# Two more row sums taken off ScalarE, and one small copy that holds the waits of four exponentials, in an attention kernel bound by TensorE

## The chip, the cores and the metric

The kernel runs on one core of a Trainium2 chip. The metric is the device time of one execution in microseconds (us), lower is better. Before the change the median of three runs is 656.49 us (655.96 to 656.77). All data is float32, apart from some bfloat16 helper tiles.

## The reference

Attention with a condition token, added to its input. Eight batches (the weights' setup names 4, but x has 8), 512 positions, 512 channels in 16 heads of 32.

```python
Q = _split_heads(x @ Wq.T + bq)
K = _split_heads(x @ Wk.T + bk)
V = _split_heads(x @ Wv.T + bv)
cQ = Q + tQ     # tQ, tK: the token, through the same weights
cK = K + tK
scores = jnp.einsum('bhqd,bhkd->bhqk', cQ, cK) / jnp.sqrt(jnp.float32(HEAD_DIM))
attn = jax.nn.softmax(scores, axis=-1)
out = jnp.einsum('bhqk,bhkd->bhqd', attn, V)
x = x + out.transpose(0, 2, 1, 3).reshape(B, S, D_MODEL)
```

## The kernel before

The work is cut into T = 32 steps t = 0 to 31: a batch times a group of four heads (one head on each 32 of the 128 partitions). The engines' instruction order is written out by hand (a manual schedule); the loop of the middle part runs over t = 1 to 28. A step has four items, here called its **quarters** i = 0 to 3. In each quarter TensorE does four things one after the other: for even t the scores of step t, keys on partitions (`exponentials`, L808 and L811); the scores of the next step's rows, queries on partitions (`row_max` with `row_scores`, L672 for even t, L664 for odd t); and either the product of the previous step's weights with V (L833) or a part of the projections of the batch ahead (L473).

The rows (u, qc) of a step u, 128 queries times four heads j, need three things. VectorE takes the negated row maximum out of PSUM (L628, L681). ScalarE takes exp(score - maximum), with the maximum as its bias (`denominators`, L729). And somebody sums each row. ScalarE can do that in the same instruction (`accum_out`), and then a second ScalarE instruction, ACTIVATION_READ_ACCUMULATOR, follows, which the profile lists under the same line.

Even and odd steps differ in what becomes of that exponential. For a **blocked** step (odd u from 1 to 27) it is kept: it is written into eight of the 14 rooms of the SBUF tile `arena`, and DMAs (`exchange`, L703) move it from there into `blocks`, 24 on the queue of SyncE and 8 on that of GpSimd in each step, half of them for the query quarters 0 and 1 and half for 2 and 3. VectorE turns blocks of 32 x 32 in place (`turn_blocks`, L692), and the result is multiplied with V. For the other steps the exponentials of the rows are thrown away after their sum, and L822 makes them again from the scores with keys on partitions; these take two rooms for each quarter. In an even step t the fourth quarter's L822 writes rooms 0 and 1, which the exchange of step t+1 has read (its first half, g = 0 and 1).

The rows of the blocked steps u = 3 to 27 are made in the even steps t = u - 1 (t = 2 to 26, thirteen of them): their row (u, 0) in the last quarter of step t - 1, and (u, 1), (u, 2), (u, 3) in the quarters 0, 1 and 2 of step t. ScalarE is a queue: behind a quarter's L822 come the four L729 of the rows, and these free the PSUM banks that a later quarter's L672 writes. Thus the exponentials of (u, 2) are read out of their banks while TensorE nears the L672 of the quarter i = 2, and those of (u, 3) before the L672 of i = 3.

Three tables say who sums the rows of blocked steps (u from 3):

```python
BY_VECTOR = {0: [(0, 0)], 1: [(2, 0), (2, 1)], 2: [(3, 0), (3, 1)]}
IN_PART = {0: (0, 1), 1: (2, 2)}
PART_AT = {0: 0, 1: 2}
```

`BY_VECTOR` names heads (qc, j) that VectorE sums from `arena` (L756) in the quarter of the key. `IN_PART` names two that GpSimd adds up in part: three adds (L746) bring 512 columns down to 128, in a free corner of the weight tile `wT_k` called `part`; VectorE then sums those 128 (L751) in the quarter that `PART_AT` gives. All other heads of the sixteen, (0,2), (0,3), the four of qc 1, (2,3), (3,2) and (3,3), are summed by ScalarE.

An instruction that has several semaphores to wait for gets separate EVENT_SEMAPHORE instructions ahead of it on its engine's queue.

Of the kernel before, what the change touches and what calls it, by code (L numbers as in the profile page):

```python
# [12 lines left out]
ALU = mybir.AluOpType  # L13
AX = mybir.AxisListType
# [3 lines left out]
def kernel(  # L18
# [38 lines left out]
    nc = tc.nc  # L57
    P = 128
# [4 lines left out]
    HG = P // HD  # L63
# [219 lines left out]
    table = const.tile([P, 1], F32, tag="table", name="table")  # L283
# [21 lines left out]
    for h in range(HG):  # L305
        r = slice(h * P, (h + 1) * P)
# [17 lines left out]
    for i in range(NS):  # L324
        r = slice(i * BL, (i + 1) * BL)
# [8 lines left out]
    def in_place(b):  # L334
# [5 lines left out]
    wT = {  # L340
        n: const.tile([P, NC, D], F32, tag=f"wT{n}", name=f"wT_{n}") for n in ("q", "k", "v")
    }
# [277 lines left out]
    sums = {}  # L620
# [66 lines left out]
    def turn_blocks(t, units):  # L687

        for n in units:
            pr = slice(n % NP * 2, n % NP * 2 + 2)  # L690
            e = blocked[t][:, :, n // NP, pr, :].rearrange("p g h s -> p g (h s)")
            nc.vector.transpose(e, e)  # L692

    def exchange(t, half):

        if t not in blocked:
            blocked[t] = room(f"blocks_{t}")
        for g in range(HG):
            for a in range(HG):
                queue = nc.gpsimd if a in BY_POOL else nc.sync  # L700
                of = arena[a * BL : (a + 1) * BL, half * HG + g, :]
                to = blocked[t][g * BL : (g + 1) * BL, a, half * 2 : half * 2 + 2]
                queue.dma_start(to.rearrange("p c h s -> p (c h s)"), of)  # L703

    APART = [(1, 1, 3), (1, 3, 3), (29, 2, 2), (29, 2, 3)]
    apart_rooms = {}
# [1 line left out]
    def denominators(t, qc, w=HG, js=range(HG)):  # L708

        if t >= T - 2:  # L710
            return
        for j in js:
            if t in BLOCKED:
                to = rows_kept(t, qc // 2)[:, :, qc % 2, j, :].rearrange(
                    "p g (c e) -> p g c e", e=BL
                )
            elif (t, qc, j) in APART:
                to = apart_rooms[j] = arena[:, (place[0] + 6) % ROOMS, j % 2 * S : j % 2 * S + S]
            else:
# [4 lines left out]
            by_vector = (  # L724
                (t, qc, j) in APART
                if t == 1 or t not in BLOCKED
                else any((qc, j) in a for a in BY_VECTOR.values()) or (qc, j) in IN_PART.values()
            )
            nc.scalar.activation(  # L729
                to,  # L730
                of,
                AF.Exp,
                bias=nmax[t][:, qc, j, :],
                **({} if by_vector else {"accum_out": sums[t][:, qc, j, :]}),
            )
            if by_vector and (qc, j) == IN_PART.get(0):
                sum_in_part(t, qc, j)

    part = wT["k"][:, 0:2, P + P // 2 : 2 * P]

    def sum_in_part(t, qc, j):

        if t in BLOCKED:
            e = rows_kept(t, qc // 2)[:, :, qc % 2, j, :].rearrange("p g (i s) -> p g i s", i=2)
            for g in range(1, HG):
                nc.gpsimd.tensor_tensor(part, part if g > 1 else e[:, 0], e[:, g], ALU.add)  # L746

    def sum_part(t, qc, j):

        if t in BLOCKED:  # L750
            nc.vector.tensor_reduce(sums[t][:, qc, j, :], part, AX.XY, ALU.add)  # L751

    def sum_by_vector(t, qc, j):

# [439 lines left out]

    def more_sums(t, i):

        for k, at in PART_AT.items():
            if at == i:
                sum_part(t + 1, *IN_PART[k])
        for qc, j in BY_VECTOR.get(i, ()):  # L1200
            sum_by_vector(t + 1, qc, j)

    for t in range(1, T - 3):
        b, r = divmod(t, G)
        blocks = t in BLOCKED
        w = 0 if blocks else HG
        items = ["V", "q", "k", "v"] if blocks else ["V", "k", "q", "v"]
        for i, item in enumerate(items):
            rows = (t + 1, i + 1) if i < 3 else (t + 2, 0)
            begin(w)  # L1210
            if not blocks:
                exponentials(t, i)
            late_first = item in ("v" if blocks else "qkv") and t % 2 == 1
            hold = row_max(*rows, late_first, w, not blocks and item in SINGLY)

            def held(i=i, hold=hold):
                hold()
                if i == 2:
                    split_max(t + 1)
                    turn_max(t + 1)  # L1220

            dens = lambda js=range(HG): denominators(*rows, w, js)
            if item in "qkv":
                products(t, item, blocks, held, dens, nothing)
            else:
                held()
                dens()
                if blocks:
                    weighted(t - 1, banks(4), banks(5), nothing)
                    released(6, 7, 0, 1, 2, 3, 5, 4)  # L1230
                else:
                    weighted(t - 1, banks(0), banks(1), lambda: more_sums(t, 0))
                    released(2, 3, 1, 4, 5, 6, 7, 0)
            if i == 0 and r % 2 == 0:
                turn_x(t + NC + 2)
                turn_x(t + NC + 3)
            if i == 0 and r == 1:
                combine_x(b + 1, 1, nc.gpsimd)
            if i == 1 and r == 0:
                combine_x(b + 1, 0, nc.gpsimd)  # L1240
            if i == 2:
                aparts[t] = masked(t)
            turn_more(t, i)
            if not blocks:
                if t == T - 4 and i == 1:
                    for j in apart_rooms:
                        nc.vector.tensor_reduce(
                            sums[t + 1][:, 2, j, :], apart_rooms[j], AX.X, ALU.add
                        )
                if i:  # L1250
                    more_sums(t, i)
                if i in IN_PART and i:
                    sum_in_part(t + 1, *IN_PART[i])
            for what in ORDERS[t % 2, i]:
                if what == "store":
                    store()
                elif what == "residual":
                    if 3 < t + 1 <= T - 4:
                        load_residual(t + 1)
                elif what == "x":  # L1260
                    load_pairs()
                elif t + 1 in BLOCKED:
                    exchange(t + 1, what)
    row_of[0] = None

    def latest_pair(of, among):
# [64 lines left out]
    t = T - 3  # L1331
# [25 lines left out]
    t = T - 2  # L1357
# [25 lines left out]
    t = T - 1  # L1383
# [61 lines left out]
    b, g = divmod(t, G)  # L1445
# [55 lines left out]
```

## Time and profile before

| | before |
|---|---|
| median of 3 runs | 656.49 us |
| the profiled execution: time, span | 656.52 us, 654.4 us |
| busy: TensorE, VectorE, ScalarE, GpSimd | 99%, 93%, 82%, 60% of the span |
| granted TensorE clock | 0.999 |
| the even step t = 14 (315.86 to 336.04), the odd one after it | 20.18 us, 18.58 us |

The span runs from the first to the last instruction; the 2.1 us between span and time lie around it. PE is TensorE's matmuls, PEld its weight loads, DVE is VectorE, ACT ScalarE, POOL GpSimd, SPq the queue of SyncE. A float32 matmul leaves two records. A row of the timeline holds the start in us, the length in us, engine, line, operation, tiles written and read, shapes and the number of instructions merged; in brackets follow the engine's idle time just before it and what ended it. Matmul records overlap, so a wait of TensorE is best seen in the time from the start of one group to the start of the next.

### The profile page before, as it was taken

To read this page: it belongs to the slowest core of one execution; us is meant where nothing else is said; L and a number is where in the kernel's file an instruction comes from. 1 tells how busy PE (TensorE), PEld (TensorE's weight loads), DVE (VectorE), ACT (ScalarE), POOL (GpSimd) and SP (SyncE) were. 2 spreads that over 40 slices of the span, in tenths; PEclk is the share of its full clock that TensorE was granted. 3 is DMA by queue.
4 is the path that set the end of the run, shared out by engine and by line. 5 is a ranking of instruction groups with operands and counts; after the bars stand their busy time and mean duration, and the time that the engine had idled before them with its cause. 6 is when DMAs were issued, how large, how long until landed. Compare 5 with 4: busy or idle time off the path is not lost.

```text
span 654.4 us, 24011 instructions
## 1 busy us (share of the span) xinstructions
PE 646.6 (99%) x9568; PEld 308.2 (47%) x9568; DVE 610.0 (93%) x911; ACT 535.5 (82%) x1298; POOL 391.6 (60%) x555
## 2 busy tenths in 40 slices
PE   8999999999999999999999999999999999999997
PEld 6444453544535454454545445454554545445432
DVE  4899999999999999999999999999999999997786
ACT  2589798888988888888989889788897988889664
POOL 4653564768647676586746766476864766555440
PEclk9999999999999999999999999999999999999999
DMA  9818549295675839758594865839567582940212
GB/s 201 159 35 214 120 105 218 62 219 129 152 176 119 210 80 212 153 130 195 95 220 93 189 159 136 200 80 221 116 158 176 123 202 49 221 106 7 53 33 33
DMA packets 140819, 90.92 MB, mean 139 GB/s; under 512 B 117436, under 2 KB 126308, under 8 KB 140708
## 3 DMA queue, kind: packets, MB, share of 16 engines
q1 hardware_dynamic: 133252, 73.91, 50.7%
q0 software_dynamic: 5568, 14.95, 9.3%
q8 instruction: 75, 1.23, 0.8%
q10 hardware_dynamic: 1888, 0.52, 0.3%
q14 instruction: 36, 0.29, 0.2%
HBM read 20.27 MB, written 8.39 MB: 44 GB/s over the span
## 4 chain that ended last, share of the span: by engine, by line
PE 97%; DMA 1%; DVE 1%; ACTq 0%; issue 0%; SPq 0%; DVEq 0%
PE psum L473 44%; PE psum L833 18%; PE psum L672 10%; PE psum L664 9%; PE psum L811 9%; PE psum L808 3%; PE psum L414 2%; DMA early<-in_x_dram 1%; PE psum L1307 1%; PE psum L1420 0%; PE psum L940 0%; PE psum L870 0%; DVE nmax L1325 0%; DVE nmax L681 0%; PE psum L792 0%; ACTq L250 0%
## 5 line engine op out<-in xcount | busy, mean ns | idle before, releaser
L628 DVE TENSOR_REDUCE nmax<-psum 128x1 f32<-128x512 f32 x326 | 204.8, 679 | 13.3 <-PE psum L672 7.9
L729 ACT ACTIVATE psum<-psum,nmax 128x512 f32<-128x512 f32 x254 | 167.8, 665 | 46.1 <-DVE nmax L628 33.9
L822 ACT ACTIVATE arena<-psum 128x512 f32<-128x512 f32 x264 | 136.3, 603 | 33.2 <-PE psum L811 26.0
L729 ACT ACTIVATE arena<-psum,nmax 128x512 f32<-128x512 f32 x226 | 146.9, 710 | 5.1 <-DVE nmax L628 3.7
L692 DVE STREAM_TRANSPOSE blocks<-blocks 128x1024 f32<-128x1024 f32 x112 | 132.2, 1217 | 0.7 <-issue 0.5
L681 DVE TENSOR_REDUCE nmax<-psum 128x2 f32<-128x1024 f32 x87 | 105.3, 1211 | 1.3 <-PE psum L672 1.3
L901 POOL TENSOR_TENSOR res<-res,recs 128x512 f32<-128x512 f32 x30 | 31.4, 1047 | 112.3 <-DVE res L900 112.3
L672 PE MATMUL psum<-kT,qT 32*128 32x512 f32 x576 | 83.1, 597 | 0.0
L833 PE MATMUL psum<-arena,v 128*32 128x512 f32 x576 | 68.5, 597 | 0.0
L811 PE MATMUL psum<-qT,kT 32*128 32x512 f32 x528 | 67.9, 587 | 0.0
L703 POOL DMA_DIRECT2D blocks<-arena x112 | 55.9, 505 | 17.7 <-PE psum L811 8.7
L664 PE MATMUL psum<-kT,qT 32*64 32x512 f32 x896 | 62.4, 613 | 0.0
L833 PE MATMUL psum<-blocks,v 128*32 128x256 f32 x896 | 52.6, 381 | 0.0
L672 PEld LDWEIGHTS psum<-kT,qT 32*128 32x128 f32 x576 | 39.4, 183 | 27.5 <-ACT arena L729 7.8
L729 ACT ACTIVATION_READ_ACCUMULATOR psum<-psum,nmax 128x1 f32 x254 | 52.3, 206 | 0.0
L756 DVE TENSOR_REDUCE sums<-arena 128x1 f32<-128x512 f32 x66 | 42.3, 673 | 0.4 <-ACT arena L729 0.4
L833 PEld LDWEIGHTS psum<-blocks,v 128*32 128x32 f32 x896 | 31.0, 110 | 20.8 <-ACT arena L822 10.6
L902 POOL TENSOR_TENSOR xr<-res,xr 128x512 f32<-128x512 f32 x30 | 38.5, 1282 | 2.4
L213 POOL TENSOR_TENSOR xr<-xr,wT_q 128x512 f32<-128x512 f32 x30 | 38.4, 1282 | 0.3
L473 PE MATMUL psum<-wT_v,xT 128*32 128x256 f32 x512 | 34.2, 382 | 0.0
L473 PE MATMUL psum<-wc_v,xc 128*32 128x256 f32 x512 | 33.5, 379 | 0.0
L833 PEld LDWEIGHTS psum<-arena,v 128*32 128x32 f32 x576 | 14.7, 110 | 38.0 <-issue 19.6
(199 smaller groups left out, 1097.8 us busy)
## 6 DMA issues: line engine op xcount, KB each, us to landing
blocks<-arena SPq DMA_DIRECT2D x336, 128.0 KB, 4.3
blocks<-arena POOLq DMA_DIRECT2D x112, 128.0 KB, 4.4
xr<-in_x_dram SPq DMA_DIRECT2D x60, 128.0 KB, 2.7
x<-in_x_dram SPq DMA_DIRECT2D x56, 128.0 KB, 2.7
out_dram<-xr SPq DMA_DIRECT2D x56, 128.0 KB, 3.1
w_q<-in_L_cond_Wq_dram SPq DMA_DIRECT2D x4, 256.0 KB
w_k<-in_L_cond_Wk_dram SPq DMA_DIRECT2D x4, 256.0 KB, 7.2
w_v<-in_L_cond_Wv_dram SPq DMA_DIRECT2D x4, 256.0 KB
```

The lines of the kernel that those rows point to most:

```text
L473: nc.tensor.matmul(pt[r], still[:, r], moving, start=(kc == kcs[0]), stop=(kc == kcs[-1]))
L628: nc.vector.tensor_reduce(nmax[t][:, qc, j : j + 1, 0], pt, AX.X, ALU.max, negate=True)
L664: nc.tensor.matmul(pt[i * n : (i + 1) * n], qkT["q", t][r, qc * P + i * n : qc * P + (i + 1) * n], qkT["k", t][r, :], start=True, stop=True,)
L672: nc.tensor.matmul(pt, qkT["q", t][r, qc * P : (qc + 1) * P], qkT["k", t][r, :], start=True, stop=True,)
L681: nc.vector.tensor_reduce(nmax[t][:, qc, pr * 2 : pr * 2 + 2, 0], pt, AX.X, ALU.max, negate=True)
L692: nc.vector.transpose(e, e)
L703: queue.dma_start(to.rearrange("p c h s -> p (c h s)"), of)
L729: nc.scalar.activation(to, of, AF.Exp, bias=nmax[t][:, qc, j, :], **({} if by_vector else {"accum_out": sums[t][:, qc, j, :]}),)
L756: nc.vector.tensor_reduce(sums[t][:, qc, j, :], rows_kept(t, qc // 2)[:, :, qc % 2, j, :], AX.XY, ALU.add)
L811: nc.tensor.matmul(bank[j], qkT["k", t][r, kc * P : (kc + 1) * P], qkT["q", t][r, :], start=False, stop=True,)
L822: nc.scalar.activation(e[:, i, :], bank[pr * 2 + i], AF.Exp)
L833: nc.tensor.matmul(pt[j * HD : (j + 1) * HD, at], vs[b % 2][:, kc, (g * HG + j) * HD : (g * HG + j + 1) * HD], e, start=(kc == chunks[0]), ...
```

## The change

Three things change, all for the blocked steps.

First, the tables. The heads (2,3) and (3,2) of the steps u = 3 to 27 are now summed in part by GpSimd, so that ScalarE's exponential of them has no `accum_out`. (2,3) gets a corner of `wT_k` of its own; (3,2) shares the one of (2,2). GpSimd adds (2,3) right behind (2,2) in the quarter i = 1, and (3,2) behind its four DMAs of the exchange's second half, in i = 2. VectorE finishes both in the quarter i = 0 of the odd step that follows, behind the transpose of the result (L900).

Second, `wait_ahead`. Behind the exponential of (u, 3, 3) ScalarE gets a copy of one column, `table` onto itself, which is made to wait for all who read or wrote the rooms 0 and 1: the eight DMAs of the exchange, GpSimd's adds, an earlier exponential. This happens in the step t = 0 too, for u = 1.

Third, `more_sums` is called in odd steps as well, and picks step and heads by the table.

```diff
-    IN_PART = {0: (0, 1), 1: (2, 2)}
-    PART_AT = {0: 0, 1: 2}
+    IN_PART = {0: [(0, 1)], 1: [(2, 2), (2, 3)], 2: [(3, 2)]}
+    PART_AT = {(0, 0): [(0, 1)], (0, 2): [(2, 2)], (1, 0): [(2, 3), (3, 2)]}
...
+    readers = []
+    def wait_ahead():
+        if readers:
+            ins = nc.scalar.copy(table, table).ins
+            for r in readers:
+                tc.add_manual_dep(
+                    ins,
+                    r.name,
+                    mybir.DependencyInfo(mybir.DependencyClass.Sync, mybir.DependencyReason.DATA),
+                    reason="rooms of the next exponentials",
+                )
+            readers.clear()
...
-                queue.dma_start(to.rearrange("p c h s -> p (c h s)"), of)
+                sent = queue.dma_start(to.rearrange("p c h s -> p (c h s)"), of)
+                if half == 0 and g < 2:
+                    readers.append(sent.ins)
...
+            if t in BLOCKED and (qc, j) == (1, HG - 1):
+                readers.append(made.ins)
+            if t in BLOCKED and (qc, j) == (3, HG - 1):
+                wait_ahead()
...
+            at = (P + P // 2, 3 * P)[j % 2 if qc else 0]
+            part_rooms[qc, j] = wT["k"][:, 0:2, at : at + P // 2]
...
-        for k, at in PART_AT.items():
-            if at == i:
-                sum_part(t + 1, *IN_PART[k])
+        u = t + 1 - t % 2
+        for qc, j in PART_AT.get((t % 2, i), ()):
+            if t > 1 or qc == 0:
+                sum_part(u, qc, j)
+        if t % 2:
+            return
...
-            if not blocks:
+            if blocks:
+                more_sums(t, i)
+            else:
...
                     exchange(t + 1, what)
+                    if what:
+                        for qc, j in IN_PART[2]:
+                            sum_in_part(t + 1, qc, j)
```

ScalarE, from the row exponentials of the quarter i = 1 of an even step (its row (u, 2)) to L822 of i = 3, before: L822 are the exponentials with keys on partitions, L729 those of the rows, `sums` in the output means a sum by ScalarE. The semaphores in brackets stand for DMAs (DMAHW on the queue of SyncE, DMASW on that of GpSimd) and engines.

```order
L729 ACTIVATE arena<-psum,nmax_3562 128x4x128 [waits DVE_49] x2
L729 ACTIVATE arena,sums_3563<-psum,nmax_3562 128x4x128 [waits DVE_49]
L822 ACTIVATE arena<-psum 128x512 [waits PE_49] x4
L729 ACTIVATE arena<-psum,nmax_3562 128x4x128 [waits DVE_49] x2
L729 ACTIVATE arena,sums_3563<-psum,nmax_3562 128x4x128 [waits DVE_49] x2
L822 ACTIVATE arena<-psum 128x512 [waits DMAHW0_49,DMASW6_49,DMAHW1_49,PE_49,DMAHW7_49,Activation_49,Pool_49]
L822 ACTIVATE arena<-psum 128x512 [waits PE_49,Activation_49]
L822 ACTIVATE arena<-psum 128x512 [waits DMAHW3_49,DMAHW2_49,DMAHW4_49,DMASW7_49,PE_49]
L822 ACTIVATE arena<-psum 128x512 [waits PE_49]
```

The same place now; L746 is the old L729, L853 the old L822, L699 the new copy.

```order
L746 ACTIVATE arena<-psum,nmax_3608 128x4x128 [waits DVE_49] x3
L853 ACTIVATE arena<-psum 128x512 [waits PE_49] x4
L746 ACTIVATE arena<-psum,nmax_3608 128x4x128 [waits DVE_49] x2
L746 ACTIVATE arena<-psum,nmax_3608 128x4x128 [waits DVE_49,Pool_49]
L746 ACTIVATE arena,sums_3609<-psum,nmax_3608 128x4x128 [waits DVE_49]
L699 COPY table<-table 128x1 [waits DMAHW1_49,DMAHW2_49,DMAHW0_49,DMAHW3_49,DMASW7_49,DMAHW4_49,DMASW6_49,DMAHW7_49,Activation_49,Pool_49]
L853 ACTIVATE arena<-psum 128x512 [waits PE_49] x4
```

The last head of the first group and the third head of the second have lost their sums, and the fourth quarter's exponentials wait for TensorE alone.

GpSimd, from the exchange's first half to its second and on, before, in an even step that also prepares the next batch (L397, L398; six of the thirteen):

```order
L703 DMA blocks_4702<-arena 32x1024 x4
L580 TENSOR_TENSOR kT_4522<-wT_k,kT_4522 128x256
L397 TENSOR_TENSOR xc<-xT_4199 128x512
L398 TENSOR_TENSOR xc<-xc,xT_4199 128x512
L746 TENSOR_TENSOR wT_k<-arena 128x2x64
L746 TENSOR_TENSOR wT_k<-wT_k,arena 128x2x64 x2
L580 TENSOR_TENSOR qT_4452<-wT_q,qT_4452 128x256
L860 TENSOR_TENSOR wT_k<-sums_4359,which 128x64
L703 DMA blocks_4702<-arena 32x1024 x4
L213 TENSOR_TENSOR xr_4627<-xr_4627,wT_q 128x16x32
L901 TENSOR_TENSOR res_4939<-res_4939,recs_4937 128x512
```

Now (L775 the adds, L718 the DMAs, L891 and L932 the old L860 and L901):

```order
L398 TENSOR_TENSOR xc<-xc,xT_4254 128x512
L775 TENSOR_TENSOR wT_k<-arena 128x2x64
L775 TENSOR_TENSOR wT_k<-wT_k,arena 128x2x64 x2
L775 TENSOR_TENSOR wT_k<-arena 128x2x64
L775 TENSOR_TENSOR wT_k<-wT_k,arena 128x2x64 x2
L580 TENSOR_TENSOR qT_4516<-wT_q,qT_4516 128x256
L891 TENSOR_TENSOR wT_k<-sums_4421,which 128x64
L718 DMA blocks_4766<-arena 32x1024 x4
L775 TENSOR_TENSOR wT_k<-arena 128x2x64
L775 TENSOR_TENSOR wT_k<-wT_k,arena 128x2x64 x2
L213 TENSOR_TENSOR xr_4691<-xr_4691,wT_q 128x16x32
L932 TENSOR_TENSOR res_5010<-res_5010,recs_5008 128x512
```

Three adds stand ahead of the second half's DMAs, and three behind them.

VectorE, at the start of an odd step, before (L681 and L628 are maxima, L900 the result's transpose):

```order
L681 TENSOR_REDUCE nmax_4358<-psum 128x2
L880 RECIPROCAL recs_4435<-psum 128x16
L900 STREAM_TRANSPOSE res_4437<-psum 128x512
L628 TENSOR_REDUCE nmax_4358<-psum 128x1 x2
L681 TENSOR_REDUCE nmax_4358<-psum 128x2
L692 STREAM_TRANSPOSE blocks_4202<-blocks_4202 128x4x256 x2
```

Now (L782 the old L751, L911 and L931 the old L880 and L900):

```order
L681 TENSOR_REDUCE nmax_4420<-psum 128x2
L911 RECIPROCAL recs_4497<-psum 128x16
L931 STREAM_TRANSPOSE res_4499<-psum 128x512
L782 TENSOR_REDUCE sums_4122<-wT_k 128x1 x2
L628 TENSOR_REDUCE nmax_4420<-psum 128x1 x2
L681 TENSOR_REDUCE nmax_4420<-psum 128x2
```

Two short sums have come in between the transpose and the maxima of the next quarter.

More of the change, by code (lines that the diff above doesn't have):

```diff
@@ L735, in denominators, with room_for_part @@
             )
[L736 removed]
+            if by_vector and (qc, j) in IN_PART[0]:
                 sum_in_part(t, qc, j)
[L739 removed]
+            if t in BLOCKED and (qc, j) == (1, HG - 1):
+                readers.append(made.ins)
+            if t in BLOCKED and (qc, j) == (3, HG - 1):
+                wait_ahead()
+    part_rooms = {}
+    def room_for_part(qc, j):
+        if (qc, j) not in part_rooms:
+            at = (P + P // 2, 3 * P)[j % 2 if qc else 0]
+            part_rooms[qc, j] = wT["k"][:, 0:2, at : at + P // 2]
+        return part_rooms[qc, j]
     def sum_in_part(t, qc, j):
         if t in BLOCKED:
+            part = room_for_part(qc, j)
             e = rows_kept(t, qc // 2)[:, :, qc % 2, j, :].rearrange("p g (i s) -> p g i s", i=2)
             for g in range(1, HG):
[L746 removed]
+                added = nc.gpsimd.tensor_tensor(part, part if g > 1 else e[:, 0], e[:, g], ALU.add)
+            if qc < 2:
+                readers.append(added.ins)
     def sum_part(t, qc, j):
         if t in BLOCKED:
[L751 removed]
+            nc.vector.tensor_reduce(sums[t][:, qc, j, :], room_for_part(qc, j), AX.XY, ALU.add)
     def sum_by_vector(t, qc, j):
@@ L1251 @@
                     more_sums(t, i)
-                if i in IN_PART and i:
-                    sum_in_part(t + 1, *IN_PART[i])
+                if i == 1:
+                    for qc, j in IN_PART[i]:
+                        sum_in_part(t + 1, qc, j)
             for what in ORDERS[t % 2, i]:
```

5 lines of the change are left out of this document (3 added, 2 removed).

## The prediction

> **What bounds the kernel now.** I read the page first, then TensorE's timeline, then the waits, then ScalarE's timeline at the places where TensorE waits. The page names TensorE:
>
> ```profile
> PE 646.6 (99%) x9568; PEld 308.2 (47%) x9568; DVE 610.0 (93%) x911; ACT 535.5 (82%) x1298; POOL 391.6 (60%) x555
> ...
> PE 97%; DMA 1%; DVE 1%; ACTq 0%; issue 0%; SPq 0%; DVEq 0%
> ```
>
> The first row has TensorE busy 99% of the span, the second gives it 97% of the chain that ended last. Read like that, no relief of ScalarE is worth anything. But a wait inside a group of matmuls hides in their overlapping records; it shows in the time from one group's start to the next one's. Here are the L672 groups of the quarters i = 1, 2 and 3 of the step t = 14, each with the group behind it, then i = 3 of the first even step (t = 2), then i = 2 and 3 of the last (t = 26) of the thirteen:
>
> ```profile
> 322.69 1.02 PE L672 MATMUL psum<-kT,qT 32*128 32x512 f32 x8
> 323.64 1.07 PE L473 MATMUL psum<-xT,wc_k 128*32 128x256 f32 x16
> 327.46 1.06 PE L672 MATMUL psum<-kT,qT 32*128 32x512 f32 x8
> 328.45 1.07 PE L473 MATMUL psum<-xT,wc_q 128*32 128x256 f32 x16
> 332.27 1.11 PE L672 MATMUL psum<-kT,qT 32*128 32x512 f32 x8
> 333.31 1.07 PE L473 MATMUL psum<-wc_v,xT 128*32 128x256 f32 x16
> ...
> 99.71 1.11 PE L672 MATMUL psum<-kT,qT 32*128 32x512 f32 x8
> 100.75 1.07 PE L473 MATMUL psum<-wc_v,xT 128*32 128x256 f32 x16
> ...
> 560.02 1.06 PE L672 MATMUL psum<-kT,qT 32*128 32x512 f32 x8
> 561.01 1.07 PE L473 MATMUL psum<-xT,wc_q 128*32 128x256 f32 x16
> 564.83 1.11 PE L672 MATMUL psum<-kT,qT 32*128 32x512 f32 x8
> 565.87 1.07 PE L473 MATMUL psum<-wc_v,xT 128*32 128x256 f32 x16
> ```
>
> The same eight records take 0.95 us in i = 1, 0.99 in i = 2 and 1.04 in i = 3, from the first even step to the last. So TensorE loses 0.04 us in i = 2 and 0.08 to 0.09 in i = 3, about 0.12 us an even step, 13 x 0.12 = 1.6 us in all. **That is all that this change can win between the steps**; in the odd steps I find no group that takes longer at one place than at another. Who is waited for:
>
> ```profile
> PEld psum L672 <- ACT arena L729: 7.8, 35, 0.2
> ...
> 327.03 0.19 PEld L672 LDWEIGHTS psum<-kT,qT 32*128 32x128 f32 x2 [0.24 <-DVE kT L578]
> 327.39 0.30 PEld L672 LDWEIGHTS psum<-kT,qT 32*128 32x128 f32 x6 [0.17 <-ACT arena L729]
> ```
>
> The first row is from the waits: the weight loads of L672 wait 35 times for ScalarE's exponentials of the blocked rows. (Its 7.8 us are idle time of the weight loader, most of which matmuls cover.) The other two are the loads in i = 2: two start at 327.03, the rest only at 327.39, released by L729. ScalarE at the same place:
>
> ```profile
> 324.80 2.44 ACT L729 ACTIVATE arena<-psum,nmax 128x512 f32<-128x512 f32 x4
> 327.08 0.26 ACT L729 ACTIVATION_READ_ACCUMULATOR arena<-psum,nmax 128x1 f32 x1
> 327.65 2.06 ACT L822 ACTIVATE arena<-psum 128x512 f32<-128x512 f32 x4 [0.31 <-PE psum L811]
> 329.58 1.87 ACT L729 ACTIVATE arena<-psum,nmax 128x512 f32<-128x512 f32 x3
> 331.29 0.25 ACT L729 ACTIVATION_READ_ACCUMULATOR arena<-psum,nmax 128x1 f32 x1
> 331.38 0.73 ACT L729 ACTIVATE arena<-psum,nmax 128x512 f32<-128x512 f32 x1
> 331.95 0.26 ACT L729 ACTIVATION_READ_ACCUMULATOR arena<-psum,nmax 128x1 f32 x1
> 332.59 2.07 ACT L822 ACTIVATE arena<-psum 128x512 f32<-128x512 f32 x4 [0.39 <-DMA blocks<-arena]
> ```
>
> The read-out of (u,2,3) ends at 327.08 + 0.26 = 327.34, and the loads go on 0.05 us later. From 327.65 on ScalarE runs without a gap through four L822, the three exponentials (u,3,0) to (u,3,2), a read-out, (u,3,3) and its read-out, which ends at 332.21 and frees the last bank for L672 of i = 3.
>
> **The change, part by part.**
>
> *The sum of (u,2,3) leaves.* Its exponential starts 0.57 us before the read-out (327.08) and lasts 0.73 (the row at 331.38), so it ends at about 327.24 instead of 327.34: the bank is free 0.09 to 0.10 us earlier, and TensorE lacked 0.04. The wait in i = 2 goes.
>
> *The sum of (u,3,2) leaves.* Three exponentials take 1.87 us, one 0.73, so a start follows a start by (1.87 - 0.73)/2 = 0.57; the third starts at 330.72 and the next at 331.38, 0.66 behind it, because of the read-out between. So (u,3,3) starts and ends 0.09 us earlier. Its own read-out stays. The chain of ScalarE from 327.65 to 332.21 hangs on L811 of i = 2, ahead of the first wait, so that wait's end doesn't move it. TensorE however comes to i = 3 0.04 earlier. It would be 0.12 earlier without both waits, the bank is 0.09 earlier: **0.09 us an even step is won, 0.03 stays as a wait**. Late next are the same exponentials, (u,3,3) with its read-out.
>
> *The copy.* Nearest to it is one column by an ACTIVATE on the same tile:
>
> ```profile
> L288 ACT ACTIVATE table<-table 128x1 f32<-128x1 f32 x1 | 0.2, 203 | 0.0
> ...
> 324.88 2.00 POOL L703 DMA_DIRECT2D blocks<-arena  x4
> ...
> blocks<-arena POOLq DMA_DIRECT2D x112, 128.0 KB, 4.4
> ```
>
> ScalarE is idle 0.39 us before L822 at 332.59, and with (u,3,3) 0.09 earlier 0.48; a copy of 0.2 us fits. What could make it late is what it waits for. GpSimd issues its two DMAs of the rooms 0 and 1 by 324.88 + 1.0 = 325.9; at the median of 4.4 us they land at 330.3, and the copy's turn comes at about 332.1. Behind it stand four L822, and TensorE waits for these. Its cost by these rows is nothing. On the other side it takes the waits off the first L822: in i = 2 L822 starts 0.19 us after the L672 group (327.65 against 327.46), in i = 3 (with seven semaphores, as the order shows) 0.32 after it (332.59 against 332.27). No group of TensorE behind it is longer for it, so I count no gain there either; the bounds are -0.1 and +0.2 us a step, and I take 0.
>
> *GpSimd's six adds a step.* Three adds cost 0.46 + 0.99 = 1.45 us:
>
> ```profile
> 369.27 0.46 POOL L746 TENSOR_TENSOR wT_k<-arena 128x128 f32<-128x128 f32 x1
> 369.80 0.99 POOL L746 TENSOR_TENSOR wT_k<-wT_k,arena 128x128 f32<-128x128 f32 x2
> 371.68 2.00 POOL L703 DMA_DIRECT2D blocks<-arena  x4
> 380.41 1.05 POOL L901 TENSOR_TENSOR res<-res,recs 128x512 f32<-128x512 f32 x1 [5.43 <-DVE res L900]
> ...
> 387.56 2.36 DVE L692 STREAM_TRANSPOSE blocks<-blocks 128x1024 f32<-128x1024 f32 x2
> ```
>
> This is t = 16, one of the six steps with L397 and L398 in the way. There the first three push the part of q (L580), the mask (L860) and the second half's four DMAs from 371.68 to about 373.1; the other three follow the DMAs. Behind, GpSimd is idle 5.43 us before L901, more than 2.9. The DMAs land 1.4 us later, at 373.1 + 2 + 4.4 = 379.5 instead of 378.1; VectorE turns the first block of the second half as the second of the two L692 in the last row, at 387.56 + 1.2 = 388.8. Cost 0; without that cover up to 1.4 us in six steps, 8.5.
>
> *VectorE's two short sums.* Each is like L751:
>
> ```profile
> 340.85 0.72 DVE L900 STREAM_TRANSPOSE res<-psum 128x512 f32<-128x512 f32 x1 [0.23 <-PE psum L833]
> 341.83 1.29 DVE L628 TENSOR_REDUCE nmax<-psum 128x1 f32<-128x512 f32 x2 [0.27 <-PE psum L664]
> ...
> 370.83 0.28 DVE L751 TENSOR_REDUCE sums<-wT_k 128x1 f32<-128x128 f32 x1
> ...
> 345.54 0.20 ACT L729 ACTIVATION_READ_ACCUMULATOR psum<-psum,nmax 128x1 f32 x1
> 347.28 1.05 PE L473 MATMUL psum<-xc,wc_k 128*32 128x256 f32 x16
> ```
>
> Two take at most 0.56 us, 0.27 are idle, so the maxima of the odd quarter i = 1 come up to 0.29 us later, and the exponentials behind them too. The last of these ends at 345.74, and its bank is written by the projection at 347.28: 1.5 us of room. VectorE has no idle time for some 10 us from there, so the delay stays for that long, but it is far below the room. Cost 0.
>
> **The sum:** 13 x 0.09 = 1.2 us off the profiled execution's 656.52, which is 655.3. That execution lies 0.03 above the median of 656.49, so the same number holds for the median. Steps 1 and 28 keep their sums by ScalarE and change by nothing.
>
> **GpSimd beside VectorE.** The adds could slow VectorE, which is 93% busy. The same product L578 once beside GpSimd's adds and L397 (t = 16) and once with GpSimd idle (t = 14):
>
> ```profile
> 369.67 0.68 DVE L578 TENSOR_TENSOR qT<-psum,qT 128x512 f32<-128x512 f32 x1
> ...
> 330.92 0.68 DVE L578 TENSOR_TENSOR qT<-psum,qT 128x512 f32<-128x512 f32 x1
> ```
>
> Equal, so I take no slowing. The Trainium skill (GPSIMD Engine Reference, 8. Key points) speaks against moving work to GpSimd: it shares its SBUF interfaces with VectorE, and contends with VectorE's instructions that have two SBUF inputs or use both ports. By that rule the adds would cost nothing here either beside maxima out of PSUM and L578 with one input in PSUM, and the two rows agree with it; it would bite only where a VectorE instruction with two SBUF inputs fell beside them.
>
> **The rivals.**
>
> *Nothing moves (0.15): 656.5.* TensorE's wait passes to another engine. For it speaks that two of the loads at 327.03 hang on VectorE (L578). Against it: they start 0.36 us before the two that wait for ScalarE, and the relief is 0.09. That the sums don't leave ScalarE at all the order excludes.
>
> *The wait goes whole (0.11): 656.52 - 13 x 0.12 = 655.0.* The bank would have to come 0.12 earlier, not 0.09; that is so if the read-out holds ScalarE longer than the starts show (0.25 us is its own length).
>
> *The copy blocks ScalarE (0.08): slower.* It is the head of a queue, and waits for both rooms at once where the third L822 waited for the second one. L822's start may slip to about 332.6 before the projection at 333.31 waits, so with 0.2 us for the copy it decides from a landing at 332.4 on, 2.1 us later than the 330.3 above. At 332.8, 2.5 us late, TensorE loses 0.4 us in each step, 13 x 0.4 = 5.2: 661.7. For it speaks that the row at 332.59 names a DMA as what ended its wait. Against it, L811 of i = 3 ends just then too, and L822 waits for that as well.
>
> **How the numbers follow.** The forecast, 655.3, has 0.66. A measurement of this kernel can tell about 0.2% from no change, 1.3 us, and the forecast's 1.2 lies just inside: I give 0.29 of its 0.66 to faster and 0.37 to the same, since the waits are read to 0.01 us in thirteen places (0.1 us in all) and medians scatter by some 0.3. The whole wait (0.11) is faster, nothing (0.15) is the same, the copy 0.06 slower and 0.02 the same. Together 0.40, 0.54 and 0.06. The range goes from 654.6, the whole wait with that scatter, to 656.5, nothing.
>
> **What would show it.** L672 to the next group at 0.95 in i = 2 and about 0.98 in i = 3; 26 read-outs of `arena` fewer; in i = 3 L822 0.19 us behind the start of L672; L900's follower L628 up to 0.3 us later with odd steps still 18.58 us. An even step of 20.09 instead of 20.18 us is the forecast. It is wrong if L672 in i = 3 stays at 1.04, if L822 of i = 3 starts later than 0.32 behind L672, or if the odd steps grow.

## The result, and the profile after

The changed kernel takes 654.72 us (median of 11 runs, 654.18 to 655.90), the kernel before beside it 656.47 (11 runs, 655.96 to 657.05). The ratio is 0.9977, with a 95% interval of 0.9970 to 0.9985, which is 1.0 to 2.0 us: a small change, but clear of no change at all. The forecast was 655.3, its range 654.6 to 656.5. The profiled execution took 655.16 us with a span of 653.3; before it was 656.52 and 654.4.

The page's first row again, then the start of the even step t = 14, the groups of L672 in i = 2 and i = 3, and the odd step behind it up to its end:

```profile
PE 645.5 (99%) x9568; PEld 308.6 (47%) x9568; DVE 613.5 (94%) x937; ACT 535.3 (82%) x1286; POOL 426.3 (65%) x633
```

```profile
315.36 0.39 PE L839 MATMUL psum<-wT_v,onesb 3*128 3x512 bf16 x4
...
326.95 1.03 PE L672 MATMUL psum<-kT,qT 32*128 32x512 f32 x8
327.91 1.07 PE L473 MATMUL psum<-xT,wc_q 128*32 128x256 f32 x16
...
331.73 1.06 PE L672 MATMUL psum<-kT,qT 32*128 32x512 f32 x8
332.71 1.07 PE L473 MATMUL psum<-wc_v,xT 128*32 128x256 f32 x16
...
335.44 1.11 PE L664 MATMUL psum<-kT,qT 32*64 32x512 f32 x16
336.49 1.06 PE L864 MATMUL psum<-arena,v 128*32 128x512 f32 x8
...
354.03 0.40 PE L839 MATMUL psum<-wT_v,onesb 3*128 3x512 bf16 x4
```

TensorE is "99% busy" as before; the shares tell nothing. The starts do: L672 to the next group takes 0.96 us in i = 2 (it was 0.99) and 0.98 in i = 3 (1.04). From L839 of i = 0 to L664 the even step takes 20.08 us, from there to the next L839 the odd one 18.59. Over the thirteen even steps the starts add up to 261.20 us, before to 262.26: 1.06 us less, about 0.08 a step, and the spans differ by 654.4 - 653.3 = 1.1. One step (t = 24) gained only 0.01, by a single longer L672 of i = 0 (1.07 us instead of 0.96); more on it at the end of the section on the prediction. What the medians show beyond 1.06 (1.75, and 1.25 in a second comparison below) is within their intervals.

Who is waited for, at the same L672 of i = 2, and how often in all:

```profile
326.53 0.62 PEld L672 LDWEIGHTS psum<-kT,qT 32*128 32x128 f32 x8 [0.24 <-DVE kT L578]
...
PEld psum L672 <- ACT arena L746: 6.8, 29, 0.2
```

All eight loads are now one row; none of them waits for ScalarE, as six did before. The second row comes from the waits: 29 times instead of 35, 6.8 us instead of 7.8.

ScalarE from the four exponentials (u,3,0) to (u,3,3) into the first ones of the next row block, (t+2,0):

```profile
329.07 2.45 ACT L746 ACTIVATE arena<-psum,nmax 128x512 f32<-128x512 f32 x4
331.36 0.26 ACT L746 ACTIVATION_READ_ACCUMULATOR arena<-psum,nmax 128x1 f32 x1
331.45 0.24 ACT L699 COPY table<-table 128x1 f32<-128x1 f32 x1
331.92 2.06 ACT L853 ACTIVATE arena<-psum 128x512 f32<-128x512 f32 x4 [0.23 <-PE psum L842]
333.85 0.70 ACT L746 ACTIVATE psum<-psum,nmax 128x512 f32<-128x512 f32 x1
...
335.08 0.24 ACT L746 ACTIVATION_READ_ACCUMULATOR psum<-psum,nmax 128x1 f32 x1
```

The four exponentials are one piece, with one read-out behind the last. The copy fits into the idle time. L853 starts 331.92 - 331.73 = 0.19 us behind L672's start (it was 0.32), and its row names TensorE as what ended the wait, no longer a DMA. (The last section shows that no DMA was waited for before either.) This 0.13 us turns out to matter. In all, ScalarE has 1286 instructions instead of 1298: 26 read-outs of `arena` fewer, as forecast, and 14 copies more.

VectorE at the start of the odd step, and GpSimd's wait for it:

```profile
340.26 0.72 DVE L931 STREAM_TRANSPOSE res<-psum 128x512 f32<-128x512 f32 x1 [0.18 <-PE psum L864]
340.90 0.43 DVE L782 TENSOR_REDUCE sums<-wT_k 128x1 f32<-128x128 f32 x2
341.25 1.28 DVE L628 TENSOR_REDUCE nmax<-psum 128x1 f32<-128x512 f32 x2
...
POOL res L932 <- DVE res L931: 82.8, 30, 5.9
```

The two short sums take the place of idle time: L628 starts 0.99 us behind the transpose, before it was 341.83 - 340.85 = 0.98. GpSimd's idle time ahead of L932 shrinks and is far from used up.

### The profile page after: what moved, and what is told of

The parts are those of the page before. It is cut to its first block, busy times and chain, and to the rows that moved or that the text cites. A ratio compares the mean times of both kernels' runs of the same rounds, so it can differ in the third digit from the quotient of the medians.

```text
span 653.3 us, 24103 instructions
## 1 busy us (share of the span) xinstructions
PE 645.5 (99%) x9568; PEld 308.6 (47%) x9568; DVE 613.5 (94%) x937; ACT 535.3 (82%) x1286; POOL 426.3 (65%) x633
## 4 chain that ended last, share of the span: by engine, by line
PE 94%; POOL 3%; DVE 1%; DMA 1%; issue 0%; ACT 0%; DVEq 0%; POOLq 0%
PE psum L473 43%; PE psum L864 18%; PE psum L672 9%; PE psum L664 9%; PE psum L842 9%; PE psum L839 3%; PE psum L414 1%; PE psum L1347 1%; DMA early<-in_L_cond_Wk_dram 1%; PE psum L1460 0%; POOL early L250 0%; PE psum L901 0%; POOL early L292 0%; ACT psum L746 0%; POOL wc_q L368 0%
## 5 line engine op out<-in xcount | busy, mean ns | idle before, releaser
L628 DVE TENSOR_REDUCE nmax<-psum 128x1 f32<-128x512 f32 x326 | 204.7, 680 | 9.6 <-PE psum L672 7.9
L746 ACT ACTIVATE psum<-psum,nmax 128x512 f32<-128x512 f32 x254 | 167.6, 663 | 46.3 <-DVE nmax L628 33.7
L853 ACT ACTIVATE arena<-psum 128x512 f32<-128x512 f32 x264 | 136.3, 602 | 32.2 <-PE psum L842 30.3
L746 ACT ACTIVATE arena<-psum,nmax 128x512 f32<-128x512 f32 x226 | 145.9, 711 | 5.0 <-DVE nmax L628 3.7
L681 DVE TENSOR_REDUCE nmax<-psum 128x2 f32<-128x1024 f32 x87 | 105.3, 1212 | 1.3 <-PE psum L672 1.3
L932 POOL TENSOR_TENSOR res<-res,recs 128x512 f32<-128x512 f32 x30 | 31.4, 1048 | 82.8 <-DVE res L931 82.8
L672 PE MATMUL psum<-kT,qT 32*128 32x512 f32 x576 | 82.2, 595 | 0.0
L718 POOL DMA_DIRECT2D blocks<-arena x112 | 55.9, 504 | 17.4 <-PE psum L842 8.7
L664 PE MATMUL psum<-kT,qT 32*64 32x512 f32 x896 | 62.4, 613 | 0.0
L775 POOL TENSOR_TENSOR wT_k<-wT_k,arena 128x128 f32<-128x128 f32 x106 | 48.5, 458 | 8.3
L672 PEld LDWEIGHTS psum<-kT,qT 32*128 32x128 f32 x576 | 39.8, 182 | 26.1 <-ACT arena L746 6.8
L746 ACT ACTIVATION_READ_ACCUMULATOR psum<-psum,nmax 128x1 f32 x254 | 51.4, 202 | 0.0
L473 PE MATMUL psum<-wT_v,xT 128*32 128x256 f32 x512 | 34.2, 382 | 0.0
L473 PE MATMUL psum<-wc_v,xc 128*32 128x256 f32 x512 | 33.5, 379 | 0.0
```

What stands on the lines that cost most here:

```text
L473: nc.tensor.matmul(pt[r], still[:, r], moving, start=(kc == kcs[0]), stop=(kc == kcs[-1]))
L628: nc.vector.tensor_reduce(nmax[t][:, qc, j : j + 1, 0], pt, AX.X, ALU.max, negate=True)
L664: nc.tensor.matmul(pt[i * n : (i + 1) * n], qkT["q", t][r, qc * P + i * n : qc * P + (i + 1) * n], qkT["k", t][r, :], start=True, stop=True,)
L672: nc.tensor.matmul(pt, qkT["q", t][r, qc * P : (qc + 1) * P], qkT["k", t][r, :], start=True, stop=True,)
L681: nc.vector.tensor_reduce(nmax[t][:, qc, pr * 2 : pr * 2 + 2, 0], pt, AX.X, ALU.max, negate=True)
L718: sent = queue.dma_start(to.rearrange("p c h s -> p (c h s)"), of)
```

## The experiments

The theory under test (A) is the prediction's: TensorE loses time only where a bank comes free late at L672; a read-out that stands ahead of that bank's release costs 0.09 us there; so (3,2) pays in i = 3, (2,3) removes a wait that the one in i = 3 takes back, and the copy is free and worth nothing. The rivals are named with each run. All steps are read as above, from starts; L672, "even" and "odd" are medians over the thirteen even steps and the odd ones behind them, in us. Lines shift by up to two between these kernels.

| | kernel | median, us (runs) | ratio to before, 95% | L672 i = 2, i = 3 | even, odd |
|---|---|---|---|---|---|
| | before | 656.16 to 656.47 | 1 | 0.987, 1.045 | 20.174, 18.586 |
| E0 | the change again | 655.12 (11) | 0.9980 (0.9971 to 0.9989) | 0.955, 0.989 | 20.087, 18.586 |
| E1 | sums without the copy | 655.41 (11) | 0.9990 (0.9981 to 0.9999) | 0.956, 0.989 | 20.088, 18.631 |
| E2 | copy alone | 656.03 (11) | 0.9996 (0.9987 to 1.0004) | 0.993, 1.044 | 20.177, 18.586 |
| E3 | (2,3) alone, copy | 656.12 (11) | 1.0002 (0.9993 to 1.0010) | 0.956, 1.079 | 20.179, 18.586 |
| E4 | (3,2) alone, copy | 655.40 (11) | 0.9989 (0.9980 to 0.9998) | 0.994, 0.955 | 20.092, 18.586 |
| E5 | (2,3), (3,2), (3,3), copy | 654.41 (6) | 0.9971 (0.9959 to 0.9983) | 0.955, 0.956 | 20.053, 18.586 |
| E7 | E5 on another chip | 654.64 (9) | 0.9975 (0.9965 to 0.9984) | 0.955, 0.956 | 20.054, 18.586 |
| E6 | (3,2), (3,3), copy | 654.70 (10) | 0.9974 (0.9964 to 0.9983) | 0.990, 0.954 | 20.088, 18.586 |
| E8 | both sums whole by VectorE | 663.02 (4) | 1.0101 (1.0086 to 1.0115) | 0.956, 0.989 | mostly 20.68; 18.59 to 19.43 |
| E9 | E5 without the copy | 655.45 (11) | 0.9988 (0.9979 to 0.9997) | 0.956, 0.970 | 20.068, 18.650 |
| E10 | three copies | 655.38 (11) | 0.9983 (0.9975 to 0.9992) | 0.956, 0.989 | 20.086, 18.623 |

E1 to E4 were compared with before in one series, E0, E5, E6 and E8 in a second on the same chip, and E7, E9 and E10 in a third on another chip. Most steps of one kernel agree to some 0.01 us; the times scatter by up to 1.8. Where two kernels lie closer than that, the steps decide, and the text says so.

**E0, the change again,** beside the kernels of the second series.

> The changed kernel once more, beside the next three on one chip. Theory A: even steps 20.09, odd 18.59, 1.1 to 1.3 us below the kernel before. Rival B (the 1.75 us first measured are the change's own): 1.6 to 1.9 below.

1.25 us faster here, with the same steps: the result repeats.

**E1, the sums without the copy.** Are the sums all of it?

```diff
-            if t in BLOCKED and (qc, j) == (3, HG - 1):
-                wait_ahead()
```

> The changed kernel without the one-column copy: the fourth quarter's exponentials wait for the DMAs themselves again. Theory A (the gain is the two read-outs alone, the copy is free and gains nothing): even steps 20.09 us as in the changed kernel, time 654.7 to 655.2, L822's successor in i = 3 starts 0.32 us behind L672 instead of 0.19. Rival B (the measured 1.75 us is more than the 1.2 counted, and the rest comes from the copy): about 0.5 us slower than the changed kernel, 655.2 to 655.4, with a longer group behind i = 3.

The even steps win what they won with the copy, but the odd steps lose 0.045 us each, 13 x 0.045 = 0.6 in all. TensorE, then ScalarE of this kernel at t = 14:

```profile
332.01 1.06 PE L672 MATMUL psum<-kT,qT 32*128 32x512 f32 x8
333.00 1.07 PE L473 MATMUL psum<-wc_v,xT 128*32 128x256 f32 x16
...
335.73 1.16 PE L664 MATMUL psum<-kT,qT 32*64 32x512 f32 x16
336.82 1.07 PE L862 MATMUL psum<-arena,v 128*32 128x512 f32 x8
```

```profile
332.33 2.07 ACT L851 ACTIVATE arena<-psum 128x512 f32<-128x512 f32 x4 [0.43 <-DMA blocks<-arena]
...
335.49 0.24 ACT L746 ACTIVATION_READ_ACCUMULATOR psum<-psum,nmax 128x1 f32 x1
```

L664 of the odd quarter i = 0 takes 336.82 - 335.73 = 1.09 us instead of 1.05. Its banks come free with the exponentials of (t+2,0); the second of these ends, with its read-out, at 335.49 + 0.24 = 335.73, just as L664 begins, and loads go on 0.05 later, as in the prediction's rows at L672: the trace has the load that waits for ScalarE's semaphore at 335.78. They are this late because L851 starts 0.32 us behind L672 again, behind its many semaphores. So A's "gain of the copy: 0" fails: it is worth half of the gain here. But the rival that made the copy the source of the gain doesn't hold alone either, as the next run shows.

**E2, the copy alone.**

```diff
-    IN_PART = {0: [(0, 1)], 1: [(2, 2), (2, 3)], 2: [(3, 2)]}
-    PART_AT = {(0, 0): [(0, 1)], (0, 2): [(2, 2)], (1, 0): [(2, 3), (3, 2)]}
+    IN_PART = {0: [(0, 1)], 1: [(2, 2)], 2: []}
+    PART_AT = {(0, 0): [(0, 1)], (0, 2): [(2, 2)]}
```

> The copy stays, the two sums go back to ScalarE. Theory A: no group of TensorE gets shorter, even steps 20.17 us, time as before the change (656.4). Rival B: 0.4 to 0.6 us faster than before, 655.9.

Nothing, in time and in steps. Before the change the exponentials of (t+2,0) were just in time, by these two rows of before, ScalarE's and TensorE's:

```profile
335.74 0.24 ACT L729 ACTIVATION_READ_ACCUMULATOR psum<-psum,nmax 128x1 f32 x1
...
336.04 1.11 PE L664 MATMUL psum<-kT,qT 32*64 32x512 f32 x16
```

335.74 + 0.24 + 0.05 = 336.03, and L664 comes at 336.04. The copy made them earlier where nobody was waiting. Once TensorE comes 0.09 earlier, there is a wait to avoid.

**E3, only (2,3) leaves,** and **E4, only (3,2) leaves,** each with the copy; the tables of E2 with that one head put back.

```diff
-    IN_PART = {0: [(0, 1)], 1: [(2, 2), (2, 3)], 2: [(3, 2)]}
+    IN_PART = {0: [(0, 1)], 1: [(2, 2), (2, 3)], 2: []}
...
-    IN_PART = {0: [(0, 1)], 1: [(2, 2), (2, 3)], 2: [(3, 2)]}
+    IN_PART = {0: [(0, 1)], 1: [(2, 2)], 2: [(3, 2)]}
```

> Only the sum of (u,2,3) leaves ScalarE; (u,3,2) goes back to it. Theory A (ScalarE's chain of i = 2 hangs on L811, ahead of the wait that goes): L672 in i = 2 falls from 0.99 to 0.955, but TensorE then arrives 0.035 us earlier at a bank that is free no earlier, and i = 3 grows from 1.04 to 1.075; even steps 20.17 us, time as before, 656.4. Rival C (each read-out is worth its half): even steps 20.13, 655.8.

> Only the sum of (u,3,2) leaves; (u,2,3) goes back to ScalarE. Theory A: L672 in i = 2 stays at 0.99, in i = 3 it falls from 1.04 to 0.95 to 0.96; even steps 20.09 us, the whole gain of the change, 654.7 to 655.3. Rival C: half the gain, 20.13 us, 655.6 to 655.8.

L672 in i = 2 and i = 3, of E3:

```profile
328.36 1.03 PE L672 MATMUL psum<-kT,qT 32*128 32x512 f32 x8
329.32 1.07 PE L473 MATMUL psum<-xT,wc_q 128*32 128x256 f32 x16
...
333.14 1.15 PE L672 MATMUL psum<-kT,qT 32*128 32x512 f32 x8
334.22 1.07 PE L473 MATMUL psum<-wc_v,xT 128*32 128x256 f32 x16
```

and of E4:

```profile
326.78 1.07 PE L672 MATMUL psum<-kT,qT 32*128 32x512 f32 x8
327.78 1.07 PE L473 MATMUL psum<-xT,wc_q 128*32 128x256 f32 x16
...
331.60 1.02 PE L672 MATMUL psum<-kT,qT 32*128 32x512 f32 x8
332.56 1.07 PE L473 MATMUL psum<-wc_v,xT 128*32 128x256 f32 x16
```

In E3 the wait of i = 2 is gone (0.96) and stands in i = 3 instead (1.08, not 1.04); the step is as long as before. In E4 i = 2 keeps its wait (1.00), i = 3 has none (0.96), and the step is as short as with both, to 0.005 us. So the sum of (2,3), with its three adds by GpSimd and one sum by VectorE a step, buys nothing by itself, and (3,2) buys all. ((2,3) pays only once nothing waits in i = 3: E5 and E6 below differ by it and by 0.035 us an even step.) This is the chain that the prediction argued from: ScalarE's time through i = 3 hangs on TensorE's blocks of i = 2, not on the end of (2,3).

**E5 and E7, (3,3) leaves as well; E6, (3,2) and (3,3) without (2,3).** Is what remains in i = 3 that last read-out? The edit of E5 and E7; E6 has the same without (2,3).

```diff
-    IN_PART = {0: [(0, 1)], 1: [(2, 2), (2, 3)], 2: [(3, 2)]}
-    PART_AT = {(0, 0): [(0, 1)], (0, 2): [(2, 2)], (1, 0): [(2, 3), (3, 2)]}
+    IN_PART = {0: [(0, 1)], 1: [(2, 2), (2, 3)], 2: [(3, 2), (3, 3)]}
+    PART_AT = {(0, 0): [(0, 1)], (0, 2): [(2, 2)], (1, 0): [(2, 3), (3, 2), (3, 3)]}
...
-            at = (P + P // 2, 3 * P)[j % 2 if qc else 0]
+            at = {(2, 3): 3 * P, (3, 3): 3 * P + P // 2}.get((qc, j), P + P // 2)
```

> The sum of (u,3,3) leaves ScalarE as well, in part by GpSimd in a third corner. Theory A: the 0.03 us that stayed in i = 3 go, L672 0.955 in all quarters, even steps 20.055 us, 0.4 us below the changed kernel; GpSimd's three more adds and VectorE's third short sum are covered. Rival D (something else is late next, VectorE's queue or GpSimd's DMAs): no gain over the changed kernel, or a loss in the odd steps.

> The sums of (u,2,3), (u,3,2) and (u,3,3) all leave ScalarE, the copy stays; here beside the two kernels that follow. Theory A (each L672 wait goes by what its bank comes free earlier): even steps 20.05 us, odd 18.586, about 0.45 us under the change by its steps, so 654.5 to 654.8. Rival B (the change's gain was all there was, and the rest of the difference is scatter of the prologue): even 20.087, 655.1.

> As the last one, but (u,2,3) is back on ScalarE. Theory A: 0.03 us stay in i = 2, nothing in i = 3; even steps 20.09 us, as the changed kernel. Rival C (each read-out is worth its part): between the changed kernel and the last one.

L672 of i = 3 in E7, from 331.21 to 332.17, is as short as anywhere:

```profile
331.21 1.03 PE L672 MATMUL psum<-kT,qT 32*128 32x512 f32 x8
332.17 1.07 PE L473 MATMUL psum<-wc_v,xT 128*32 128x256 f32 x16
```

With three sums gone and the copy in place no L672 waits in any quarter of the usual step, and the even step is 20.053, 0.12 under before: the prediction's "all that can be won". This kernel is the fastest of the study, by its median (654.41) 0.7 us under E0 in the same series; but the intervals overlap with the change's, and the steps put it 13 x 0.033 = 0.4 us below. E6 keeps the wait of i = 2 and has the change's steps: with either pair of heads one wait of about 0.03 stays.

**E8, the two sums whole by VectorE,** at the same place, without GpSimd.

```diff
-    IN_PART = {0: [(0, 1)], 1: [(2, 2), (2, 3)], 2: [(3, 2)]}
-    PART_AT = {(0, 0): [(0, 1)], (0, 2): [(2, 2)], (1, 0): [(2, 3), (3, 2)]}
+    IN_PART = {0: [(0, 1)], 1: [(2, 2)], 2: []}
+    WHOLE = [(2, 3), (3, 2)]
+    PART_AT = {(0, 0): [(0, 1)], (0, 2): [(2, 2)]}
...
-                else any((qc, j) in a for a in BY_VECTOR.values()) or any((qc, j) in a for a in IN_PART.values())
+                else any((qc, j) in a for a in BY_VECTOR.values()) or any((qc, j) in a for a in [*IN_PART.values(), WHOLE])
...
+            for qc, j in WHOLE if i == 0 and t > 1 else ():
+                sum_by_vector(u, qc, j)
```

> The sums of (u,2,3) and (u,3,2) go to VectorE whole, 512 columns each in the quarter i = 0 of the odd step, where the change puts two short sums. Theory A with VectorE's queue: its maxima come 0.85 us later than in the changed kernel, and VectorE has no idle time until the next even step; the odd steps stay at 18.59 us (1.2 us of room and more), but L672 of i = 0 in the even step has 0.5 us of room: it grows by 0.3 to 0.4 us, 4 to 5 us in all, 659. Rival E (VectorE, 94% busy, has idle time enough): as the changed kernel, 655.

6.6 us slower than before, more than A expected. The two whole sums of an odd step, three exponentials of ScalarE at the end of that step, which wait for VectorE's maxima (L629), then TensorE's loads and groups in i = 0 of the next even step (from 318.22):

```profile
305.09 1.24 DVE L788 TENSOR_REDUCE sums<-arena 128x1 f32<-128x512 f32 x2
...
316.12 1.95 ACT L747 ACTIVATE arena<-psum,nmax 128x512 f32<-128x512 f32 x3 [0.18 <-DVE nmax L629]
...
319.84 0.29 PEld L673 LDWEIGHTS psum<-kT,qT 32*128 32x128 f32 x2 [0.18 <-ACT v L545]
...
319.31 1.65 PE L673 MATMUL psum<-kT,qT 32*128 32x512 f32 x8
320.89 0.64 PE L865 MATMUL psum<-blocks,v 128*32 128x256 f32 x8
```

1.24 us stand where the short sums took 0.43. The loss lies in the next even step's L672 of i = 0 (here L673), which takes 1.58 us instead of 0.96: two of its loads wait for a copy of `v` (L545), which stands in ScalarE's queue behind exponentials that wait for VectorE's maxima. It is 0.6 us in nine of the thirteen even steps (0.3 in a tenth), and four odd steps are 0.4 to 0.8 us longer, because the even step behind them begins with a wait for a DMA of the maxima (`wT_v<-split`, 0.3 to 0.8 us); that is more than expected. VectorE, 94% busy, has little idle time to make such a delay up. So at this place the two sums are free only because GpSimd shortens them first.

**E9, three sums without the copy,** E5 with E1's edit. Does the loss of E1 grow with what is won?

> The same three sums leave ScalarE, but without the copy. The four exponentials of i = 3 follow the transposed blocks of L842, so they follow TensorE's own pace, and start 0.32 us behind L672 again as without the copy before. Theory A: the loss of the odd steps is then the same as without the copy before, 18.632 instead of 18.586, 0.6 us in all, beside even steps of 20.05: about 655.0 to 655.2. Rival B (ScalarE's pace through i = 3 is fixed by what stands ahead of it, and what TensorE wins in the even step it loses at L664 of the odd one): odd about 18.665, 655.5, no better than two sums without the copy.

```profile
332.05 1.03 PE L672 MATMUL psum<-kT,qT 32*128 32x512 f32 x8
333.02 1.07 PE L473 MATMUL psum<-wc_v,xT 128*32 128x256 f32 x16
...
335.75 1.18 PE L664 MATMUL psum<-kT,qT 32*64 32x512 f32 x16
336.86 1.06 PE L862 MATMUL psum<-arena,v 128*32 128x512 f32 x8
```

```profile
332.37 2.07 ACT L851 ACTIVATE arena<-psum 128x512 f32<-128x512 f32 x4 [0.53 <-DMA blocks<-arena]
...
335.53 0.24 ACT L746 ACTIVATION_READ_ACCUMULATOR psum<-psum,nmax 128x1 f32 x1
...
333.02 0.59 PEld L473 LDWEIGHTS psum<-wc_v,xT 128*32 128x32 f32 x16 [0.77 <-ACT arena L851]
```

The first rows are TensorE's, then two of ScalarE's and TensorE's loads for the projection behind L672. L664 loses 0.065 us, not 0.045, and L672 of i = 3 has 0.015 back: together 13 x 0.08 = 1.0 us over E7, and 655.45 is no better than E1's 655.41. That is the rival's result. L851 does stand 0.32 behind L672, as A had it; but this is L672's start, and the third sum shortens L672 itself, behind that point. Against E1 it takes 0.989 - 0.970 = 0.019 off L672, and L664 loses 0.065 - 0.045 = 0.020 more: even and odd step together are 38.72 us in both. Without the copy the third sum is worth nothing. The 0.015 hang on the same late start: the first exponential of L851 ends at 332.97 (it lasts 0.60), and the projection L473, whose loads wait for it, comes 0.05 later, at 333.02. In E7 L853 starts 0.13 earlier, and L473 waits for nothing there.

**E10, three copies.** Does the gain by the copy lie in when L853 starts, or in where the waits are handled?

```diff
+            for _ in range(2):
+                nc.scalar.copy(table, table)
             readers.clear()
```

> The changed kernel with two more one-column copies behind the one that holds the waits. Each is a record of 0.24 us, and ScalarE waits 0.23 us for TensorE ahead of the first L853 of i = 3. Theory A (the gain by the copy is the earlier start of these exponentials): the extra copies fill that idle time and more, L853 starts 0.3 us or more behind L672 instead of 0.19, L664 of the odd i = 0 waits again, odd steps 18.63 to 18.70, 655.5 to 656.5 in all. Rival B (the gain by the copy is that the waits are handled there, and ScalarE has room to spare): odd steps stay at 18.586, 655.1.

```profile
331.56 0.24 ACT L699 COPY table<-table 128x1 f32<-128x1 f32 x1
331.84 0.41 ACT L708 COPY table<-table 128x1 f32<-128x1 f32 x2
332.16 2.06 ACT L855 ACTIVATE arena<-psum 128x512 f32<-128x512 f32 x4
...
335.31 0.24 ACT L748 ACTIVATION_READ_ACCUMULATOR psum<-psum,nmax 128x1 f32 x1
```

```profile
331.84 1.06 PE L672 MATMUL psum<-kT,qT 32*128 32x512 f32 x8
...
335.56 1.15 PE L664 MATMUL psum<-kT,qT 32*64 32x512 f32 x16
336.64 1.07 PE L866 MATMUL psum<-arena,v 128*32 128x512 f32 x8
```

The waits sit on the first copy as in the change, but two further copies push the exponentials back to 332.16, again 0.32 behind L672, and most of the loss is back: odd steps of 18.623. So it is the start that counts. One rule gives all the odd steps, here at t = 14: L664 waits until 0.05 us after the second read-out of (t+2,0). E1: 335.73 + 0.05 - 335.73 = 0.05 (measured 0.045). E9: 335.77 + 0.05 - 335.75 = 0.07 (0.065). E10: 335.55 + 0.05 - 335.56 = 0.04 (0.037). The change: 335.32 + 0.05 = 335.37, before 335.44, no wait.

## Why the prediction held, and where its sizes were off

*What bounds the kernel* held: only waits inside L672 could be won, 0.12 us an even step. E7 wins just that (20.174 - 20.054) and nothing further.

*The two sums* held to 0.01 us: 0.96 and 0.98 to 0.99 at L672, 20.087 an even step where 20.09 was forecast, against 20.174 before. That (2,3) alone moves its wait to i = 3 and (3,2) alone wins 0.09 was the step's logic, and E3 and E4 show it. "Late next are the same exponentials, (u,3,3) with its read-out" held too (E5, E7), but was not the whole answer: the exponentials of (t+2,0), just in time before, came next as well.

*The copy at 0* was right as a cost and wrong as a gain. That L822 would move from 0.32 to 0.19 behind L672 was forecast and came; the step "no group of TensorE behind it is longer for it, so I count no gain there either" failed, because it asked the kernel before, in which the odd L664 had no wait, and not the kernel with the sums gone. The term is a gain of 0.045 us a step, 0.6 in all, half of the whole (E1), still inside the bounds of -0.1 to +0.2. The sum came out right because the forecast counted the relief of L672 in full and never charged the wait at L664 that the copy prevents. Two omissions cancelled, and to that extent the total was right by luck.

*GpSimd's adds at 0* held. Its idle time ahead of the result's product was, by the waits of before,

```profile
POOL res L901 <- DVE res L900: 112.3, 30, 5.9
```

and is 82.8 us now, so cover was left. *VectorE's two sums* were taken as up to 0.29 us late and came 0.01 late: their records overlap (0.43 us for two, where 2 x 0.28 was taken), and the idle 0.27 swallows them. The cost of 0 held in the usual step, but not because of the 1.5 us of room in the odd step that the prediction relied on: in E8 a delay smaller than that room cost 0.6 us in the next even step, at the L672 of i = 0, which the prediction did not look at. And it did not hold everywhere. At two places of the changed kernel TensorE waits for exponentials, or a copy of `v` behind them, that had waited for VectorE's maxima: 0.03 to 0.04 us in i = 1 of the step t = 5 and 0.11 in i = 0 of t = 24. Both profiles of this kernel (the first and E0's) show them, the one of before doesn't. Whether the two short sums or TensorE's earlier arrival bring them about isn't separated.

*GpSimd beside VectorE*: no slowing beyond 0.01 us showed. In the changed kernel 23 of VectorE's single maxima (L628) ran beside GpSimd's adds, at 0.68 us in the median, and those with GpSimd idle took 0.67.

*The rivals*: the copy didn't block ScalarE (in all thirteen even steps it runs without idle time ahead of it), and the sums did move the step. (The loads that the prediction has waiting for ScalarE at 327.39 are six by its row, not two; its argument stands.) The whole wait (655.0) didn't go, although the first median, 654.72, lies nearer to it: the steps show 0.08 to 0.09 of the 0.12 and the rest at L672 of i = 3.

What stays open: why single executions of one kernel differ by up to 1.8 us. The usual steps don't; the time up to the first odd step does (64.3 to 64.8 us in most profiles, 65.6 in E3's; 64.8 and 64.3 for the same kernel in E5 and E7), and most profiles have a longer group at a few single places (0.02 to 0.36 us), some of which, like those at t = 5 and t = 24, come back in the next profile of the same kernel. No run here was made to settle that.

## What to carry to other kernels

Read an engine that is "99% busy" by the starts of equal groups: 0.03 to 0.09 us of waiting per group stood in no share and in almost no row. Ask what is late next in the kernel with the change in it, not in the one before: chains that were just in time (here by 0.01 us) begin to bind as soon as the engine that they feed gets faster. Where an instruction on such a chain has many semaphores, let an idle moment ahead of it carry them, and look at how far it then starts behind its last input.

## What the runs showed of the hardware

An exponential with seven semaphores started 0.32 us behind TensorE's L672, the same one with a single semaphore 0.19 us (E1 against the change). The traces show where the 0.13 us go. They also record the EVENT_SEMAPHORE instructions that the timeline leaves out, and the numbers are the same to 0.003 us in all thirteen even steps, before the change and in E1. TensorE's semaphore is given 0.17 us behind the start of L672. The EVENT_SEMAPHORE that holds it ends at 0.20; behind it on ScalarE's queue stands another one with two further semaphores, from 0.24 to 0.27, and the exponential starts at 0.32. That other one takes 0.04 us, as long as those whose semaphores had been given long before, so nothing was waited for there. In the change TensorE's semaphore comes at 0.17 as well, it is the only one, and the exponential starts at 0.19. So it is the handling of semaphores already given, behind the last one to come, that costs the 0.13 us, and not a late DMA, although the row of before names one.

A read-out has a record of 0.19 to 0.26 us but holds the next exponential back by only 0.09, and so the bank behind it: L672 in i = 3 takes 1.08 us with the read-out of (3,2) and 0.99 without it (E3 and the change). A copy of one column took 0.24 us alone; in a row of three a start followed a start by 0.28 and 0.22.
